# A graph layer's first attention group: node row and edge sources in one table, and one gather to a block instead of two

## The chip, the cores and the metric

The kernel runs on one core of a Trainium2 chip. The metric is the device time of one execution in microseconds (us); the time of the kernel before is the median of three runs. A profile is one execution recorded by the hardware profiler, with its own, longer time. The engines are named as in the profile: PE (matrix multiply), PEld (its weight loads), DVE (vector engine), ACT (scalar engine), POOL (GpSimd, which here issues all indirect DMAs), SP (the sync engine, which issues the plain DMAs). Each engine takes its instructions in program order, and so do POOL and SP with the DMAs that they issue.

## What is computed

A graph layer on 6,250 nodes with 256 features and 206,250 directed edges sorted by their destination. It adds to x an edge attention (8 heads of 32) and a linear attention, then a mixture of 8 experts with a capacity. The edge attention, which the change touches, is this (reference, cut):

```python
q = (feats @ Wq.T + bq).reshape(bs, NHEAD, HDIM).transpose(1, 0, 2)   # k, v likewise
r, c = (edge_index[:, 0], edge_index[:, 1])        # source, destination
sim = jnp.einsum('hed,hed->eh', q[:, c, :], k[:, r, :]) * scale
m = jax.ops.segment_max(sim, c, num_segments=bs)
p = jnp.exp(sim - m[c])
s = jax.ops.segment_sum(p, c, num_segments=bs)
attn = p / s[c]
agg = jax.ops.segment_sum(attn.T[..., None] * v[:, r, :], c, num_segments=bs)   # axes moved in the original
return agg @ Wo.T + bo
...
xn = _layernorm(x, axis=-1)
x = x + _L0_gnn_ref(xn, ...) + _L0_mix_ref(xn[None], ...)[0]
x = x + _L0_ffn_ref(_layernorm(x, axis=-1)[None], ...)[0]
```

For every node the rows k and v of its in-edges' sources (33 on average) have to be fetched; that is what the many gathers are for.

## The kernel before

**Blocks and groups.** The nodes are cut into 49 natural blocks of 128 (NB; one node to a partition). They form three groups of 21, 17 and 11 blocks (GROUPS). Within a group the nodes are sorted by falling number of edges, so that a sorted block needs few slots more than its nodes have edges. SLOTS holds the planned number of slots of each block: 62, 43, 41 and down to 24 in the first group, 725 slots there, 1,714 in all.

**The prologue** (L382 to L578) walks the natural blocks b = 0 to 48. For each: two matmuls give the block's k and v rows (L548, `rows_of(b + 2)`), DVE scales them into a tile kv (L562, one of six buffers of pool ap6), and SP stores kv into the DRAM table kv_tab (L565). After every fourth block SP also loads the next rows of x and of the transposed x (`load_x`, L409 and L213), and ACT takes the sums for the layer norm. Beside it `index_step(b)` (L528) finds where each node's edges begin. The edge list is cut into rows of 62 entries. For a set of 7 blocks (GB) POOL gathers one such row for each node (`row_gathers`, L504, tile part, two buffers), DVE counts the entries below the node's number (`in_rows`, L515 to L519) and writes the node's first edge into st_nat. The sets are handled at b = 8, 13, 18, ... (`due`); at the step for set k the gathers for set k + 2 are issued. From b = 24 on, `rank_group(0)` sorts the first group's nodes, one step to a block; its end (L371 to L378) gives, for each sorted place, the node (node_ri, node_x), its first edge (start_ri), its number of edges (deg_r) and its norm (rstd_r).

**The attention loop** (L1602 to L1655) goes over the sorted blocks in `order`, in units of at most 20 slots, each in chunks of at most 5 slots. For each chunk DVE multiplies the gathered k by the queries (L1621) and reduces (L1622); one unit later it weighs v (L1550) and PE sums it into pa (L1554). Jobs of the other stages (sorting the later groups, linear attention, routing, experts) are put between by a planned pace (`background`).

**The gathers.** `gather_to` (L648) runs six chunks ahead of DVE. For each slot of a chunk POOL issues one indirect DMA of 128 rows of 2 KB from kv_tab into a chunk buffer kvg (L662; RING = 10 buffers). When a block begins, it first issues two gathers for the block after it: `sources` (L600) fetches the sources of its edges from the list src, as many as it has slots, into idx (L605; pool cp3, three buffers); `queries` (L611) fetches the nodes' rows of x into the upper half of qs (L615; pool cp4, four buffers). The kv gathers take their row numbers from idx; `query_steps` makes the queries from qs.

**Waits and lanes.** In the built program each DMA carries one of eight completion lanes of its queue, taken in turn, and the next DMA of a lane waits until the last one of it is complete. A buffer that is written again waits, on the issuing engine, for whoever read it last; a read of an index tile by a gather counts as ended when that gather is complete.

Of the kernel before, what the change touches and what calls it, by code (L numbers as in the profile page):

```python
# [9 lines left out]
F32 = mybir.dt.float32  # L10
BF16 = mybir.dt.bfloat16
I32 = mybir.dt.int32
# [6 lines left out]
P = 128  # L19
# [9 lines left out]
GROUPS = (21, 17, 11)  # L29
# [15 lines left out]
def planned_slots(n_nodes, n_edges, groups):  # L45

    lam = max(1.0, n_edges / n_nodes - 1.0)  # L50
    pm = [math.exp(-lam)]
    for k in range(1, 1000):
        pm.append(pm[-1] * lam / k)
    more = [sum(pm[k:]) for k in range(len(pm))]
    out, b0 = [], 0
    for g in groups:
        m = min(n_nodes - b0 * P, g * P)
        for j in range(g):
            k = 1
            while True:  # L60
                p = more[k]
                if (m * p <= 0.005) if j == 0 else (m * p + 2.0 * math.sqrt(m * p * (1 - p)) <= P * j):
                    break
                k += 1
            out.append(k)
        b0 += g
    return out
# [3 lines left out]
def gps_layer(  # L71
# [36 lines left out]
    nc = tc.nc  # L108
    N, D = x.shape
    E = n_edges  # L110
    NB = -(-N // P)
# [16 lines left out]
    SMAX = max(SLOTS)  # L128
# [11 lines left out]
    dram = ctx.enter_context(tc.tile_pool(name="dram", bufs=1, space=DRAM))  # L140
# [5 lines left out]
    xbufs = [dram.tile([TILES[g] * SIZE[g], XW], F32, name=f"xbuf{g}") for g in range(NG)]  # L146

    rbufs = [dram.tile([TILES[g] * SIZE[g], D], F32, name=f"rbuf{g}") for g in range(NG - 1)]

    agg_tab = dram.tile([NB * P, D], F32, name="agg_tab")  # L150
    xbuf = dram.tile([NX * C + NB * P, D], F32, name="xbuf")
# [5 lines left out]
    with tc.manual_schedule():  # L157
# [24 lines left out]
        st_nat = keep.tile([P, NB + 1], F32, name="st_nat")  # L182
        nc.vector.memset(st_nat, float(E))
        node_ri = keep.tile([P, NB], I32, name="node_ri")
        node_x = keep.tile([P, NB], I32, name="node_x")
# [31 lines left out]
        cp4 = mctx.enter_context(tc.tile_pool(name="c4", bufs=4))  # L217
        cp3 = mctx.enter_context(tc.tile_pool(name="c3", bufs=3))
        cp2 = mctx.enter_context(tc.tile_pool(name="c2", bufs=2))
# [50 lines left out]
        GB = 7  # L270
# [111 lines left out]
        with ExitStack() as actx:  # L382
            ap1 = actx.enter_context(tc.tile_pool(name="a1", bufs=1))
            ap2 = actx.enter_context(tc.tile_pool(name="a2", bufs=2))
# [69 lines left out]
            first_i = di[:, :TW].rearrange("p (r w) -> p r w", w=RW)[:, :, 0]  # L454
# [38 lines left out]
            def rows_of_nodes():  # L493
                nc.vector.tensor_tensor_scan(cnt1, ones[:, :NB], pc[:, 1, :], 0.0, op0=ALU.mult, op1=ALU.add)
                nc.vector.tensor_sub(cnt1, cnt1, pc[:, 1, :])
                nc.vector.tensor_add(cnt1, cnt1, pc[:, 0, :])
                nc.vector.tensor_scalar(cnt1, cnt1, -1.0, 0.0, op0=ALU.add, op1=ALU.max)
                nc.vector.tensor_copy(row_i, cnt1)
                nc.vector.tensor_scalar(cnt1, cnt1, float(RW), None, op0=ALU.mult)

            def row_gathers(b0):
                part = ap2.tile([P, GB, RW], I32, name="part")
                for b in range(b0, min(NB, b0 + GB)):
                    nc.gpsimd.indirect_dma_start(  # L504
                        out=part[:, b - b0, :], out_offset=None, in_=row_dst,
                        in_offset=bass.IndirectOffsetOnAxis(ap=row_i[:, b : b + 1], axis=0),
                    )
                got.append(part)

            def in_rows(b0):  # L510
                g = slice(b0, min(NB, b0 + GB))
                n = g.stop - b0
                part = got.pop(0)
                below = ap1.tile([P, GB, RW], F32, name="below")
                nc.vector.tensor_tensor(  # L515
                    below[:, :n, :], part[:, :n, :], node[:, g, None].to_broadcast([P, n, RW]), ALU.is_lt
                )
                nc.vector.tensor_reduce(cnt2[:, g], below[:, :n, :], AX.X, ALU.add)
                nc.vector.tensor_add(st_nat[:, g], cnt1[:, g], cnt2[:, g])  # L519
# [4 lines left out]
            due = {8 + 5 * k: k for k in range(NSET)}  # L524
            ranks = rank_group(0, rc, ap1, ap2)
            late_sets = []

            def index_step(b):  # L528
                if b == 1:
                    rows_of_nodes()  # L530
                    row_gathers(0)
                    row_gathers(GB)
                if b in due:
                    k = due[b]
                    in_rows(k * GB)
                    if k + 2 < NSET:
                        row_gathers((k + 2) * GB)
                if b >= 8 + 5 * (need0 - 1) + 1:
                    next(ranks, None)

# [14 lines left out]
            for b in range(NB):  # L555
                k = b // GX
                if b % GX == 0 and k + 1 < NGX:
                    stat_square(k + 1)
                if b % GX == GX - 1 and k + 1 < NGX:
                    stat_end(k + 1)  # L560
                kv = ap6.tile([P, 2 * D], F32, name="kv")
                nc.vector.scalar_tensor_tensor(  # L562
                    kv, done.pop(b), rstd[:, b : b + 1], bn, op0=ALU.mult, op1=ALU.add
                )
                nc.sync.dma_start(kv_tab[b * P : (b + 1) * P, :], kv)  # L565
                if b % GX == GX - 1 and k + 1 < NGX:
                    load_x(k + 3)
                    if k + 2 < NGX:
                        stat_sum(k + 2)
                rows_of(b + 2)  # L570
                if b == 4:
                    less_mean(wq, D)
                index_step(b)
# [13 lines left out]
            for b in order:  # L587
# [3 lines left out]
                for i in range(n_p):  # L591
                    n = cut[i + 1] - cut[i]
# [5 lines left out]
            idx_of, qs_of, kv_of = {}, {}, {}  # L598

            def sources(i):  # L600
                if i < NB:
                    b = order[i]
                    S = SLOTS[b]
                    idx = cp3.tile([P, SMAX], I32, name="idx")
                    nc.gpsimd.indirect_dma_start(  # L605
                        out=idx[:, :S], out_offset=None, in_=src[:, :],
                        in_offset=bass.IndirectOffsetOnAxis(ap=start_ri[:, b : b + 1], axis=0),
                    )
                    idx_of[b] = idx

            def queries(i):  # L611
                if i < NB:
                    b = order[i]
                    qs = cp4.tile([P, 2 * D], F32, name="qs")
                    nc.gpsimd.indirect_dma_start(  # L615
                        out=qs[:, D:], out_offset=None, in_=x[:, :],
                        in_offset=bass.IndirectOffsetOnAxis(ap=node_x[:, b : b + 1], axis=0),
                    )
                    qs_of[b] = qs

            def query_steps(b):
# [26 lines left out]
            def gather_to(k):  # L648

                nonlocal pool_at  # L650
                while pool_at < min(k, len(chunk_list)):
                    u, c = chunk_list[pool_at]
                    b, part, _, _, _, chunks = units[u]
                    i = order.index(b)
                    if c == 0 and part == 0 and i > 0:
                        sources(i + 1)
                        queries(i + 1)
                    j0, j1 = chunks[c]
                    kv = kvp.tile([P, W, 2 * D], F32, name="kvg")
                    kv_of[u, c] = kv  # L660
                    for j in range(j0, j1):
                        nc.gpsimd.indirect_dma_start(  # L662
                            out=kv[:, j - j0, :], out_offset=None, in_=kv_tab[:, :],
                            in_offset=bass.IndirectOffsetOnAxis(ap=idx_of[b][:, j : j + 1], axis=0),
                        )
                    pool_at += 1

            for i in range(2):
                sources(i)
                queries(i)  # L670
# [931 lines left out]
        for u, (b, part, n_p, s0, s1, chunks) in enumerate(units):  # L1602
            n = s1 - s0
# [621 lines left out]
```

## Time and profile before

| | |
|---|---|
| median of three runs | 2770.39 us (2766.16 to 2770.42) |
| profiled execution | 3178.49 us, of which the span from first to last instruction is 3176.7 us |
| mean granted PE clock in it | 0.846 |
| busy share of the span | PE 71%, DVE 69%, POOL 59%, PE loads 54%, ACT 24% |
| DMA, software queue (POOL's gathers) | 148,880 packets, 477.59 MB, 50.3% of 16 engines' span |
| DMA, hardware queue (SP's) | 108,220 packets, 231.24 MB, 20.7% |
| idx gathers (L605) | 49, from 114.3 to 2880.5 us, 944 ns each |
| query gathers (L615) | 49, from 115.6 to 2881.8 us, 946 ns each |
| row gathers of the prologue (L504) | 49, busy 46.41 us of POOL |

The profile's columns: a group of equal instructions stands as line, engine, operation, written tile <- read tiles, count, busy us and mean ns of one, then the idle time of the engine just before them and what ended most of it ("issue": nothing that the profile shows; "remote": something outside the engines' own instructions). [...] The profiled execution is 408 us longer than the median, so a stage's length in it is not its length in the runs. The page's own chain of waits names only the last few instructions, 0% of the span, so the reading goes by stages: the prologue to 140 us, the first group to about 1290 us, the later groups to about 2890 us, and the rest.

### The profile page before, as it was taken

Reading aid. Unit: us, or ns where it says so; the run is one execution under the profiler, and the core shown is the slowest. Engines: PE = TensorE matmul, PEld = TensorE weight load, DVE = VectorE, ACT = ScalarE, POOL = GpSimd, SP = SyncE. Lnnn points to the kernel's source line nnn. Section 1 sums busy time; section 2 is a strip of 40 time slices with the busy share of each in tenths; the row PEclk is TensorE's granted clock in tenths of the full one; section 3 lists DMA queues with packets and bytes.
Section 4 is the critical chain, followed back from the end, with each engine's and each line's share of the span. In section 5 each row is a group of like instructions: output and inputs, shape, how many; then the busy total and the mean of one; then the engine's idle time right before and its main releaser. Section 6 shows DMA issues by size and latency. Waiting matters only on the chain. (4 is left out here: it accounts for less than half of the span.)

```text
span 3176.7 us, 29837 instructions
## 1 busy us (share of the span) xinstructions
PE 2247.2 (71%) x8968; PEld 1721.8 (54%) x8968; DVE 2183.7 (69%) x3637; ACT 767.7 (24%) x2022; POOL 1870.1 (59%) x2026
## 2 busy tenths in 40 slices
PE   7636577767767567674548888889844479999847
PEld 3324344545545445553337677777633357777637
DVE  4758788878778668787947666666867546766621
ACT  5200233333333212220012222222200112222113
POOL 4356666666666655656676566666665665655411
PEclk9857788888889778887769899989967689999969
DMA  7556777777776666766687778777765778887475
GB/s 233 188 166 183 214 225 223 238 215 232 219 218 196 191 186 208 216 186 170 195 273 266 238 260 268 247 266 257 216 170 177 247 252 269 275 274 265 156 265 209
DMA packets 257274, 710.88 MB, mean 224 GB/s; under 512 B 42183, under 2 KB 92113, under 8 KB 245580
## 3 DMA queue, kind: packets, MB, share of 16 engines
q0 software_dynamic: 148880, 477.59, 50.3%
q1 hardware_dynamic: 108220, 231.24, 20.7%
q8 instruction: 76, 1.25, 0.2%
q14 instruction: 98, 0.80, 0.1%
HBM read 626.63 MB, written 82.06 MB: 223 GB/s over the span
## 5 line engine op out<-in xcount | busy, mean ns | idle before, releaser
L662 POOL DMA_INDIRECT kvg<-kv_tab,idx x1714 | 1628.5, 950 | 1024.3 <-issue 470.8
L1554 PE MATMUL pa<-kvg,ident 128*128 128x256 f32 x3428 | 1015.1, 452 | 578.0 <-DVE kvg L1550 374.6
L1554 PEld LDWEIGHTS pa<-kvg,ident 128*128 128x128 f32 x3428 | 758.0, 228 | 795.8 <-DVE kvg L1550 424.1
L1621 DVE TENSOR_TENSOR kvg<-kvg,qc 128x1024 f32<-128x1024 f32 (+1 forms) x381 | 513.7, 1348 | 104.4 <-issue 45.4
L1622 DVE TENSOR_REDUCE sim<-kvg 128x32 f32<-128x1024 f32 (+1 forms) x381 | 515.3, 1353 | 17.8 <-remote 4.7
L1550 DVE TENSOR_TENSOR kvg<-kvg,pr 128x1024 f32<-128x1024 f32 (+1 forms) x381 | 510.2, 1342 | 0.0
L1370 PE MATMUL bank<-xTe,wt 128*128 128x256 f32 x1088 | 269.0, 394 | 12.5 <-ACT xTe L1360 7.5
L1387 PE MATMUL bank<-wt,hTe 128*128 128x256 f32 x1088 | 266.8, 393 | 11.7 <-issue 11.7
L1370 PEld LDWEIGHTS bank<-xTe,wt 128*128 128x128 f32 x1088 | 212.7, 198 | 47.4 <-issue 9.3
L1387 PEld LDWEIGHTS bank<-wt,hTe 128*128 128x128 f32 x1088 | 211.6, 197 | 45.7 <-issue 16.5
L1376 ACT ACTIVATE hTe<-bank,wt 128x256 f32<-128x256 f32 x272 | 112.7, 470 | 319.0 <-PE bank L1370 131.6
L756 PE MATMUL bank<-wm,xTm 128*128 128x512 f32 x392 | 182.0, 608 | 0.9 <-issue 0.9
L1404 ACT ACTIVATE res<-bank,xt 128x256 f32<-128x256 f32 x68 | 32.2, 473 | 366.5 <-PE bank L1393 144.3
L756 PEld LDWEIGHTS bank<-wm,xTm 128*128 128x128 f32 x392 | 73.9, 199 | 74.6 <-issue 74.5
L1561 DVE TENSOR_REDUCE s<-pr 128x8 f32<-128x120 f32 (+8 forms) x108 | 30.4, 281 | 118.2 <-ACT pr L1653 71.4
L1579 DVE TENSOR_TENSOR acc<-acc,pa 128x256 f32<-128x256 f32 x59 | 24.9, 421 | 124.2 <-remote 99.5
L548 PE MATMUL pkv<-wn,xT 128*128 128x512 f32 x196 | 94.0, 632 | 14.2 <-issue 11.2
L765 ACT ACTIVATE sq<-bank 128x512 f32<-128x512 f32 x98 | 55.4, 594 | 199.7 <-PE pa L1554 72.5
L785 ACT ACTIVATE ck<-bank,rk 128x64 f32<-128x64 f32 x392 | 86.4, 350 | 29.3 <-DVE rk L782 12.5
L1407 DVE TENSOR_TENSOR res<-res,xt 128x256 f32<-128x256 f32 x79 | 33.3, 421 | 82.9 <-ACT res L1404 62.1
L773 DVE TENSOR_REDUCE rv<-sq 128x16 f32<-128x1024 f32 x49 | 59.4, 1212 | 43.1 <-ACT sq L765 37.8
L896 PE MATMUL bank<-ident,qs 128*128 128x128 f32 x56 | 14.2, 343 | 95.2 <-DVE qs L1587 40.2
(312 smaller groups left out, 2467.2 us busy)
## 6 DMA issues: line engine op xcount, KB each, us to landing
wt<-in_w_rows_dram SPq DMA_DIRECT2D x34, 1152.0 KB
wt<-in_w_rows_dram SPq DMA_DIRECT2D x34, 1028.0 KB
kvg<-kv_tab,idx POOLq DMA_INDIRECT x1714
xbuf<-zero SPq DMA_DIRECT2D x43, 514.0 KB
kvg<-in_w_rows_dram SPq DMA_DIRECT2D x11, 1152.0 KB
kv_tab<-kv SPq DMA_DIRECT2D x49, 256.0 KB
hx_tab<-hx SPq DMA_DIRECT2D x49, 256.0 KB
kvg<-in_w_rows_dram SPq DMA_DIRECT2D x11, 1028.0 KB
```

Of the source, the lines that this page charges most:

```text
L548: nc.tensor.matmul(done[b], xTs[b // GX][:, b % GX, c, :], wn[:, c, :], start=(c == 0), stop=(c == DC - 1))
L662: nc.gpsimd.indirect_dma_start(out=kv[:, j - j0, :], out_offset=None, in_=kv_tab[:, :], in_offset=bass.IndirectOffsetOnAxis(ap=idx_of[b][: ...
L756: nc.tensor.matmul(pm, xT_of[b][:, c, :], wmf[:, c, s * MI : (s + 1) * MI], start=(c == 0), stop=(c == DC - 1),)
L773: nc.vector.tensor_reduce(rv, sqs[b], AX.X, ALU.add)
L785: nc.scalar.activation(cks[b][:, h, :], pms[b][0][:, h * MD : (h + 1) * MD], AF.Copy, scale=rk[:, h : h + 1])
L1370: nc.tensor.matmul(ph[:, k, :], w[:, c, f * P : (f + 1) * P], T[t]["xT"][:, c, :size], start=(k == 0 and c == 0), stop=(k == 1 and c == DC ...
L1376: nc.scalar.activation(T[t]["hT"][:, f, :size], ph[:, k, :], AF.Relu, bias=w1_t[:, V1 + f : V1 + f + 1])
L1387: nc.tensor.matmul(py, T[t]["hT"][:, f, k * P : (k + 1) * P], w[:, f, :], start=(f == 0), stop=(last and f == FC - 1),)
L1550: nc.vector.tensor_tensor(vals, vals, v["pr"][:, j0 - s0 : j1 - s0, :, None].to_broadcast([P, m, GH, GD]), ALU.mult)
L1554: nc.tensor.matmul(v["pa"], ident, kv[:, j, D:], start=(j0 + j == s0), stop=(j0 + j == s1 - 1),)
L1621: nc.vector.tensor_tensor(keys, keys, qc[:, None, :].to_broadcast([P, j1 - j0, D]), ALU.mult)
L1622: nc.vector.tensor_reduce(sim[:, j0 - s0 : j1 - s0, :], keys.rearrange("p j (h d) -> p j h d", d=GD), AX.X, ALU.add)
```

## The change

The first group's two gathers to a block become one. A new DRAM table xs_tab has a row for each node of the first 21 natural blocks: its 256 values of x, and behind them the IW = 62 sources that begin at its first edge (1,272 bytes in all). It is filled in the prologue. The x part is one DMA from DRAM to DRAM (2,688 rows), issued by SP just ahead of the first kv store. The sources come in three sets of 7 blocks, at b = 8, 13 and 18: once a set's first edges are in st_nat, DVE copies them to integers (first_i, two buffers), POOL gathers 62 sources for each node, block by block (ids, one buffer of 7 blocks), and SP stores ids into the table's last columns. These gathers stand on POOL behind the row gathers of the same step, and the store stands on SP behind the kv store of the same step.

In the first group `sources` does nothing any more, and `queries` fetches a row of xs_tab into a wider qs; its last 62 columns serve as idx. The later groups keep both gathers, but idx now has two buffers (cp2) in place of three (cp3). In the built program the first gather of a set of ids waits for DVE's copy and, from the second set on, for the store of the set before it; the store waits for all the set's gathers; and 26 of the 28 remaining idx gathers wait on several or all of the eight lanes of POOL's queue, where they waited on one.

```diff
--- before.py
+++ after.py
@@ -146,6 +146,9 @@
     xbufs = [dram.tile([TILES[g] * SIZE[g], XW], F32, name=f"xbuf{g}") for g in range(NG)]
 
     rbufs = [dram.tile([TILES[g] * SIZE[g], D], F32, name=f"rbuf{g}") for g in range(NG - 1)]
+
+    IW = max(planned_slots(N, E, GROUPS)[: GROUPS[0]])
+    xs_tab = dram.tile([GROUPS[0] * P, D + IW], F32, name="xs_tab")
 
     agg_tab = dram.tile([NB * P, D], F32, name="agg_tab")
     xbuf = dram.tile([NX * C + NB * P, D], F32, name="xbuf")
@@ -524,6 +527,24 @@
             due = {8 + 5 * k: k for k in range(NSET)}
             ranks = rank_group(0, rc, ap1, ap2)
             late_sets = []
+            nc.sync.dma_start(xs_tab[:, :D], x[: GROUPS[0] * P, :])
+
+            def first_sources(b0):
+
+                g = slice(b0, min(GROUPS[0], b0 + GB))
+                n = g.stop - b0
+                first_i = ap2.tile([P, GB], I32, name="first_i")
+                nc.vector.tensor_copy(first_i[:, :n], st_nat[:, g])
+                ids = ap1.tile([P, GB, IW], I32, name="ids")
+                for i in range(n):
+                    nc.gpsimd.indirect_dma_start(
+                        out=ids[:, i, :], out_offset=None, in_=src[:, :],
+                        in_offset=bass.IndirectOffsetOnAxis(ap=first_i[:, i : i + 1], axis=0),
+                    )
+                nc.sync.dma_start(
+                    xs_tab[b0 * P : (b0 + n) * P, D:].rearrange("(t p) w -> p t w", p=P),
+                    ids[:, :n, :].bitcast(F32),
+                )
 
             def index_step(b):
                 if b == 1:
@@ -535,6 +556,8 @@
                     in_rows(k * GB)
                     if k + 2 < NSET:
                         row_gathers((k + 2) * GB)
+                    if k * GB < GROUPS[0]:
+                        first_sources(k * GB)
                 if b >= 8 + 5 * (need0 - 1) + 1:
                     next(ranks, None)
 
@@ -598,10 +621,10 @@
             idx_of, qs_of, kv_of = {}, {}, {}
 
             def sources(i):
-                if i < NB:
+                if GROUPS[0] <= i < NB:
                     b = order[i]
                     S = SLOTS[b]
-                    idx = cp3.tile([P, SMAX], I32, name="idx")
+                    idx = cp2.tile([P, SMAX], I32, name="idx")
                     nc.gpsimd.indirect_dma_start(
                         out=idx[:, :S], out_offset=None, in_=src[:, :],
                         in_offset=bass.IndirectOffsetOnAxis(ap=start_ri[:, b : b + 1], axis=0),
@@ -611,11 +634,19 @@
             def queries(i):
                 if i < NB:
                     b = order[i]
-                    qs = cp4.tile([P, 2 * D], F32, name="qs")
-                    nc.gpsimd.indirect_dma_start(
-                        out=qs[:, D:], out_offset=None, in_=x[:, :],
-                        in_offset=bass.IndirectOffsetOnAxis(ap=node_x[:, b : b + 1], axis=0),
-                    )
+                    row = cp4.tile([P, 2 * D + IW], F32, name="qs")
+                    qs = row[:, : 2 * D]
+                    if i < GROUPS[0]:
+                        nc.gpsimd.indirect_dma_start(
+                            out=row[:, D:], out_offset=None, in_=xs_tab[:, :],
+                            in_offset=bass.IndirectOffsetOnAxis(ap=node_ri[:, b : b + 1], axis=0),
+                        )
+                        idx_of[b] = row[:, 2 * D :].bitcast(I32)
+                    else:
+                        nc.gpsimd.indirect_dma_start(
+                            out=qs[:, D:], out_offset=None, in_=x[:, :],
+                            in_offset=bass.IndirectOffsetOnAxis(ap=node_x[:, b : b + 1], axis=0),
+                        )
                     qs_of[b] = qs
 
             def query_steps(b):
```

## The prediction

> **What bounds the kernel now.** First the page's list of groups, for the dearest line, then the busy time by stage. The columns of the second view are the stretch, its length, busy us (and instructions) of PE, PE loads, DVE, ACT and POOL, the granted clock, the DMA share and GB/s.
>
> ```profile
> L662 POOL DMA_INDIRECT kvg<-kv_tab,idx x1714 | 1628.5, 950 | 1024.3 <-issue 470.8
> ```
>
> ```profile
> 0.00:140.00 140.00, 108.63 (x298) 51.26 (x298) 81.05 (x195) 61.23 (x213) 52.73 (x62) 0.95 0.64 212
> 140.00:1290.00 1150.00, 747.70 (x2668) 537.23 (x2668) 895.68 (x1454) 314.28 (x822) 738.03 (x779) 0.82 0.70 208
> 1290.00:2890.00 1600.00, 1186.62 (x4926) 958.97 (x4926) 1090.17 (x1733) 321.26 (x774) 990.93 (x1075) 0.86 0.74 237
> ```
>
> A gather costs POOL 0.95 us of work and 0.30 us until the next may start (470.8 us of "issue" over 1454 waits): 1.25 us. With that, POOL is taken for 738 + 779 x 0.30 = 972 of the first group's 1150 us, 85%; DVE is busy for 78%. So who waits for whom? DVE's waits in the first group (total, times, longest):
>
> ```profile
> DVE acc L1579 <- remote: 56.9, 10, 8.1
> ...
> DVE kvg L1621 <- DMA kvg<-kv_tab,idx: 6.7, 3, 4.9
> ```
>
> DVE waited only 6.7 us for gathered rows, 4.9 of it for the very first chunk. The gathers run ahead; POOL itself waits for buffers, also in the later groups:
>
> ```profile
> POOL kvg L662 <- issue: 240.6, 774, 3.7
> POOL kvg L662 <- PE pa L1554: 130.7, 47, 8.7
> POOL kvg L662 <- remote: 72.9, 29, 4.8
> ```
>
> So POOL is not last in the attention loop: DVE, in step with PE and ACT, is. The prologue is different. The timeline (start, length, engine, line, what; in brackets the idle time before):
>
> ```profile
> 47.22 0.94 POOL L504 DMA_INDIRECT part<-in_dst_dram,row_i  x1 [0.30 <-issue]
> 53.93 0.94 POOL L504 DMA_INDIRECT part<-in_dst_dram,row_i  x1 [5.77 <-DVE below L515]
> ...
> 114.35 0.94 POOL L605 DMA_INDIRECT idx<-in_src_dram,start_ri  x1 [18.59 <-DVE rstd_r L377]
> ...
> 138.06 1.08 POOL L662 DMA_INDIRECT kvg<-kv_tab,idx  x1 [18.86 <-issue]
> ```
>
> The first kv gather stands still for 18.86 us although its sources were asked for at 114.35: it needs all of kv_tab, whose last store SP issued at 135.06. The stores of the 49 kv blocks (L562, L565) set the prologue's end, and all that follows starts from there.
>
> **Gathers removed in the first group.** 21 idx gathers go (L605; 944 ns and a gap of 0.30 each): 21 x 1.25 = 26 us of POOL. Two of them stand at 114 to 119 us, ahead of the wait to 138: worth 0. The others give POOL more of the slack that it already has. Bounds: 0, and -26 if POOL were last everywhere. By the 6.7 us that DVE waits for rows: 0. The row that is now fetched is longer (1,272 bytes for 1,024), but a gather of 248 bytes (L504, 0.94), of 1,024 (L615, 946 ns) and of 2,048 (L662, 950 ns) cost POOL the same, so it costs nothing there.
>
> The Trainium skill, "DMA: Bandwidth & Descriptors", section "Anatomy of one DMA — SWDGE (gpsimd) path", gives a fixed cost of about 2.0 us for each DMA whatever its size. By that, half as many query and source gathers would bring 21 x 2.0 = 42 us. But that is latency, and these are issued a whole block, some 33 gathers, before they are read; by the rows it is 1.25 us of an engine that waits anyway. I take the rows.
>
> **Gathers added in the prologue.** 21 ids gathers, in three sets of 7 behind the row gathers of the steps at b = 8, 13 and 18: 7 x 1.25 = 8.75 us of POOL each. Before, POOL has the next row set from 39.7 to 48.2 and only then idles. As built the order is: third row set to 48.5, ids 0 to 57.2, fourth row set to 66, ids 1 to 74.7, fifth row set to 83.5, ids 2 to 92.2, back to back. When do they land? The first chunk shows it:
>
> ```profile
> 141.95 0.95 POOL L662 DMA_INDIRECT kvg<-kv_tab,idx  x1 [0.30 <-issue]
> ...
> 145.70 1.22 DVE L1621 TENSOR_TENSOR kvg<-kvg,qc 128x1024 f32<-128x1024 f32 x1 [4.89 <-DMA kvg<-kv_tab,idx]
> ```
>
> The chunk's last gather left POOL at 142.90, and its reader started 2.8 us later. So the sets are in SBUF at 60, 77.5 and 95.
>
> **The store of ids, on SP: the term that decides.** Each set is written to xs_tab by a DMA in SP's queue, in program order: behind the kv store of b = 8, 13 or 18, ahead of the next ones. It must wait for its 7 gathers, and behind it wait kv stores 9 to 13, 14 to 18 and 19 onwards, and the loads of x and xT. SP is blocked from about 36 to 60, 63 to 77.5 and 80 to 95. kv has six buffers (ap6), so DVE gets six blocks past the last stored one: block 25 needs the store of block 19, which goes out at 95 and lands near 98. In the trace of before:
>
> ```profile
> 76.56 1.41 DVE L562 SCALAR_TENSOR_TENSOR kv<-pkv,rstd,bn 128x512 f32<-128x512 f32 x2
> ```
>
> These are blocks 24 and 25; block 25 starts at 77.2. That is 98 - 77 = 21 us late. Blocks 26 to 35 carry the rank steps of the first group with DVE 18.75 of 20 us busy (80 to 100 us), and 36 to 48 come every 1.72 us, PE's own pace, so nothing is caught up: **+21 us**. Bounds: if the prologue outside the profile runs at PE's pace from 13.4 us on, block 25 stands near 62 before and the loss is 36; if POOL issues without the gap, its 56 gathers from 22 take 53 us instead of 70 and the loss is about 5. I take 21, the row's.
>
> The rule that speaks against the change is on the same page and section: DMA engines do not wait on semaphores, the issuing sequencer does, before dispatch. If instead a DMA could be queued with its wait, SP would pass on and only POOL's 26 us would count; its last row set is read at b = 38 (117.8 us) and would land at about 113, so the sum would be 0. In the trace SP's waits are those of the rule (45.0 us at L565 for kv), so I take 21.
>
> **x into xs_tab.** One DRAM-to-DRAM DMA of 2.75 MB on SP, ahead of the first kv store. Between 115 and 120 us the DMAs moved 372 GB/s; at that rate it is 7.4 us of all engines. Below: 0, since it falls into 11 to 25 us, partly idle, and its backlog of kv stores lies under the SP block from 36 on. Above: 15, if reading and writing DRAM halves the rate. I take 0; the three copies of first_i (DVE, under 0.2 us each) are 0 under the same block.
>
> **Two idx buffers for three, in the groups after the first.** The gather into idx for block i+1 now reuses the buffer whose readers are the kv gathers of block i-1, issued just before it. As built it waits for all eight completion lanes (two blocks: for four or six), that is for every gather under way; before it waited for one lane. 26 of the 28 blocks have it: 2.8 - 0.3 = 2.5 us of POOL each, 65 us. Queued behind are the idx and query gathers and the next chunk's kv gathers, and DVE's L1621 waits for these. Cover: POOL's waits for buffers, 130.7 + 72.9 us and smaller ones, in a run-ahead of some five chunks of 8 us. Bounds 0 and +65; since DVE met missing rows at about 8 of some 200 chunks there, I take **+5**.
>
> **Sum** against the profiled execution: 3178.5 us (span 3176.7 and 1.8 around it) + 21 + 5 = 3204. The median of the runs is 2770.4, 408 us less, and I add the same 26 us: what is added is issue and landing time. **2796 us.**
>
> **The rivals.**
> - POOL is the bound outside the profile (22%). From 140 to 2890 POOL is taken for 1729 + 1854 x 0.30 = 2285 us; if the missing 408 us all come out of these 2750, POOL is at 98%. Against it: DVE's waits. Then the first group gains some 20 of its 26 us, the idx waits cost 50 of their 65, the prologue 25: 2825.
> - The faster one: POOL paces the first group alone, with its relief worth the whole 26 us, while the later idx waits stay hidden. It decides once the prologue's block costs under 26; at 10, because gathers issue quicker without the profile: 2770 - 26 + 10 = 2754 (9%). For it: 85% taken; against: three waits of DVE for rows.
> - The store on SP is hidden (9%): kv_tab is not what ends the prologue outside the profile, +3 remains: 2773. Against: 18.86 us at L662.
>
> The forecast has 60%. **Chances**, with 0.2% (5.5 us) as what a measurement can tell from none: faster 9, within 8, slower 83 of 100. The range is 2762 to 2852: below, part of the faster case; above, the POOL case with its terms at 36 and 65.
>
> **What would show it.** Right: in the timeline of after, SP's store of ids issued at about 60, 77 and 95; block 25 of kv near 98; first kv gather near 159; POOL's idx rows with a wait of about 2.5 us. Wrong: the first kv gather at 138 to 145, DVE waiting tens of us for gathered rows, or the first group shorter by 20 us or more.

## The result, and the profile after

The changed kernel takes 2856.5 us (median of 4 runs, 2854.53 to 2859.08) where the kernel before takes 2770.4 (4 runs, 2766.16 to 2770.6): a ratio of 1.0321, 95% interval 1.0309 to 1.0334. It is slower by 86 us; 26 were forecast.

Two things about the times come first. The profiled execution of the changed kernel took 2854.66 us, within the range of its runs: recording a profile costs no time that can be seen. And the kernel before needed 3,177 to 3,213 us in four of the five series of experiments below and 2,768 us in one. Each series ran on one chip, and these were five different ones. So the trace that the prediction read (3178.49 us) was hardly the runs' execution made longer by the recorder; it matches the chips on which this program needs some 400 us more. Below, **chip B** is the one of 2,768 us, which agrees with the runs of the result (2770.4; which chip those ran on is not recorded), and A1 to A4 are the others (3,213, 3,204, 3,177 and 3,208 us). Ratios are always taken within a series.

The timeline of the changed kernel, first SP's DMAs around the first store of ids (start, length, queue, line, what):

```profile
37.13 0.33 SPq L588 DMA_DIRECT2D kv_tab<-kv  x1
58.04 0.38 SPq L544 DMA_DIRECT2D xs_tab<-ids  x1
58.51 1.48 SPq L588 DMA_DIRECT2D kv_tab<-kv  x3
...
75.45 0.37 SPq L544 DMA_DIRECT2D xs_tab<-ids  x1
...
93.03 0.37 SPq L544 DMA_DIRECT2D xs_tab<-ids  x1
93.51 0.51 SPq L588 DMA_DIRECT2D kv_tab<-kv  x1
94.06 0.44 SPq L412 DMA_DIRECT2D kvg<-in_x_dram  x1
```

SP sends nothing for 20 us ahead of 58.04 and then three kv stores at once. DVE and ACT in the same stretch (in brackets the idle time before, and what ended it), and POOL's first kv gather:

```profile
62.41 0.75 DVE L585 SCALAR_TENSOR_TENSOR kv<-pkv,rstd,bn 128x512 f32<-128x512 f32 x1 [16.23 <-DMA kv_tab<-kv]
...
101.40 0.42 ACT L439 ACTIVATE junk<-kvg 128x256 f32<-128x256 f32 x1 [12.56 <-DMA kvg<-in_x_dram]
...
103.56 0.17 DVE L443 TENSOR_SCALAR sums<-sums 128x4 f32<-128x4 f32 x1 [10.91 <-ACT junk L439]
103.64 1.41 DVE L585 SCALAR_TENSOR_TENSOR kv<-pkv,rstd,bn 128x512 f32<-128x512 f32 x2
```

```profile
163.32 1.14 POOL L693 DMA_INDIRECT kvg<-kv_tab,qs  x1 [21.71 <-DMA kv_tab<-kv]
```

So the block on SP reaches DVE first through the six kv buffers, as forecast (16.23 us). At the second and third store it comes by another path: the rows of x that SP loads behind the store (94.06 us) arrive late, ACT's sums wait for them, and DVE for the sums. From 30 to 163 us DVE waits 17.7 us for kv buffers and 33.4 us for these sums. The kv gathers start at 163.3. What the page says of the remaining idx gathers, and of the time in which a gather lands:

```profile
L628 POOL DMA_INDIRECT idx<-in_src_dram,start_ri x28 | 26.5, 947 | 126.4 <-DMA kvg<-kv_tab,idx 85.6
...
kvg<-kv_tab,idx POOLq DMA_INDIRECT x989, 4.6
```

28 instructions of 0.947 us have 126.4 us of idle time ahead of them. The trace puts 85.6 of it down to gathers under way, whose median is 4.6 us from issue to landing, and 37.0 to nothing that it names. By the waits of the built program, 26 of the 28 wait for gathers under way.

### The profile page after: what moved, and what is told of

It reads as the page before. It is cut to its first block, busy times and chain, and to the rows that moved or that the text cites. A ratio compares the mean times of both kernels' runs of the same rounds, so it can differ in the third digit from the quotient of the medians.

```text
span 2852.8 us, 29942 instructions
## 1 busy us (share of the span) xinstructions
PE 2161.2 (76%) x8968; PEld 1669.6 (59%) x8968; DVE 2181.2 (76%) x3640; ACT 771.8 (27%) x2022; POOL 1871.4 (66%) x2026
## 3 DMA queue, kind: packets, MB, share of 16 engines
q8 instruction: 76, 1.25, 0.2%
## 5 line engine op out<-in xcount | busy, mean ns | idle before, releaser
L1585 PE MATMUL pa<-kvg,ident 128*128 128x256 f32 x3428 | 972.8, 438 | 470.7 <-DVE kvg L1581 470.2
L693 POOL DMA_INDIRECT kvg<-kv_tab,idx x989 | 941.3, 952 | 349.8 <-issue 256.9
L1585 PEld LDWEIGHTS pa<-kvg,ident 128*128 128x128 f32 x3428 | 727.1, 218 | 674.3 <-DVE kvg L1581 540.7
L693 POOL DMA_INDIRECT kvg<-kv_tab,qs x725 | 688.2, 949 | 251.5 <-issue 173.3
L1418 PE MATMUL bank<-wt,hTe 128*128 128x256 f32 x1088 | 257.8, 384 | 0.0
L1401 PE MATMUL bank<-xTe,wt 128*128 128x256 f32 x1088 | 254.5, 380 | 1.4 <-ACT xTe L1391 1.4
L1401 PEld LDWEIGHTS bank<-xTe,wt 128*128 128x128 f32 x1088 | 205.4, 191 | 30.0 <-ACT xTe L1391 1.9
L628 POOL DMA_INDIRECT idx<-in_src_dram,start_ri x28 | 26.5, 947 | 126.4 <-DMA kvg<-kv_tab,idx 85.6
L571 PEld LDWEIGHTS pkv<-wn,xT 128*128 128x128 f32 x196 | 39.9, 213 | 86.1 <-DVE kv L585 43.7
L507 POOL DMA_INDIRECT part<-in_dst_dram,row_i x49 | 46.5, 949 | 48.5 <-DVE cnt L502 20.1
```

The costliest lines, as they stand in the source:

```text
L571: nc.tensor.matmul(done[b], xTs[b // GX][:, b % GX, c, :], wn[:, c, :], start=(c == 0), stop=(c == DC - 1))
L693: nc.gpsimd.indirect_dma_start(out=kv[:, j - j0, :], out_offset=None, in_=kv_tab[:, :], in_offset=bass.IndirectOffsetOnAxis(ap=idx_of[b][: ...
L1401: nc.tensor.matmul(ph[:, k, :], w[:, c, f * P : (f + 1) * P], T[t]["xT"][:, c, :size], start=(k == 0 and c == 0), stop=(k == 1 and c == DC ...
L1418: nc.tensor.matmul(py, T[t]["hT"][:, f, k * P : (k + 1) * P], w[:, f, :], start=(f == 0), stop=(last and f == FC - 1),)
L1585: nc.tensor.matmul(v["pa"], ident, kv[:, j, D:], start=(j0 + j == s0), stop=(j0 + j == s1 - 1),)
```

## The experiments

From here a run is read by **stages**: to the first kv gather (the prologue), the first group (725 kv gathers), the second, the third, and the rest. Stages are taken from the start times of the gathers in the trace.

### The third index buffer

E1, e6, e14 and e17 are the changed kernel with idx in three buffers again, on four chips; e5 is the changed kernel itself beside e6. E2 and e15 are the kernel before with two buffers, and nothing else of the change. E0, e4 and e13 are the kernel before, profiled for its stages.

```diff
-                    idx = cp2.tile([P, SMAX], I32, name="idx")
+                    idx = cp3.tile([P, SMAX], I32, name="idx")
```

> The kernel before, unchanged, for a second profile: its first one took 3178 us where the runs take 2770, while the changed kernel's profile (2855) agrees with its runs. Theory (the added time is the SP block in the prologue plus the idx waits of the later groups): a span near 2770, the first kv gather at about 115 to 120 us, so that the changed kernel's 163 is some 45 us late, and the first group as long in both. Rival (the loss lies in the first group, in the gathers that now hang on a longer row): the first kv gather near 138 as in the first profile, and a first group some 40 us shorter than in the changed kernel.

> The changed kernel with three idx buffers again. Theory: the 26 waits of about 4 us for all gathers under way go, and with them half of the loss: 2857 becomes about 2815. Rival (these waits are hidden behind the buffers, as my prediction had it): about 2850. A first kv gather at 163 in both.

> The kernel before with two idx buffers and nothing else. Now 46 or so of 49 blocks have the wait. Theory: 40 us for 26 blocks gives about 70 for 46, so 2840, less if the first group has more slack than the later ones (2810). Rival (hidden): 2770 to 2778.

> The kernel before, profiled beside the next three so that its stages can be set against theirs on the same chip. Both theories: the first row gather of the attention loop starts at 137 to 139 us, and the first group then takes about 1,140 us on a chip that runs the kernel in 3,200 us, or about 970 us on one that runs it in 2,770 us.

> The changed kernel as it is. Theory A (three terms: the prologue loses about 25 to 32 us, the first group gains about 26 us because 21 gathers of 1.25 us leave POOL there and POOL paces it, and two index buffers cost 40 to 85 us in the later groups): 50 to 90 us over before, ratio 1.016 to 1.033. Theory B (what I predicted: prologue +21, later groups +5, first group 0): ratio 1.009.

> The changed kernel with three index buffers again, beside the changed kernel on one chip. Theory A: the later groups get back 40 to 85 us, ratio to before 0.998 to 1.004. Theory B: only 5 us come back, ratio 1.007.

> The kernel before, profiled. On a chip that runs it in about 2,770 us: first row gather at 115 to 123 us, first group 964 to 970 us, second and third together about 1,485 us. On one that runs it in about 3,200 us: 138 to 146 us and 1,135 to 1,150 us.

> The changed kernel with three index buffers. Theory A (two buffers cost the second and third group about 65 us where the chip is fast): 60 to 70 us under the changed kernel, 20 to 27 us over before, ratio 1.007 to 1.010 on a chip of 2,770 us; on one of 3,200 us 1.001 to 1.004. Theory B (what I predicted, 5 us for the buffers): 1.025 to 1.03 on the fast chip.

> The kernel before with two index buffers in place of three, and nothing else of the change. 47 blocks meet the drain instead of 26. Theory A: 26 blocks cost 65 us, so 47 cost 95 to 120 us, ratio 1.034 to 1.043 on a chip of 2,770 us (1.014 to 1.026 on one of 3,200 us, as measured). Theory B (5 us for 26): under 10 us, ratio under 1.004.

> The changed kernel with three index buffers. On a chip that runs the kernel before in about 2,770 us: Theory A (two buffers cost the later groups 65 us there) 2,785 to 2,797 us, ratio 1.006 to 1.010; Theory B (5 us) 2,845 to 2,855 us, ratio 1.027 to 1.031. On a chip of 3,200 us: 1.000 to 1.004 as before.

| kernel | chip | ratio to before (95%) | prologue | first | second | third | rest |
|---|---|---|---|---|---|---|---|
| before (e0) | A1 | one run | 137.8 | 1148.8 | 1007.1 | 723.3 | 203.7 |
| three idx (e1) | A1 | 1.0015 (0.9995 to 1.0035) | 169.9 | 1121.6 | 999.1 | 716.6 | 206.3 |
| before, two idx (e2) | A1 | 1.0203 (1.0142 to 1.0264) | 146.1 | 1179.6 | 1027.7 | 720.9 | 208.6 |
| before (e4) | A2 | one run | 145.9 | 1145.2 | 995.8 | 714.2 | 203.5 |
| changed (e5) | A2 | 1.0134 (1.0102 to 1.0165) | 170.0 | 1121.5 | 1019.1 | 730.5 | 200.4 |
| three idx (e6) | A2 | 1.0028 (1.0010 to 1.0046) | 172.4 | 1119.5 | 988.5 | 720.0 | 208.5 |
| before (e13) | A3 | one run | 144.3 | 1138.8 | 997.0 | 702.1 | 203.4 |
| three idx (e14) | A3 | 1.0014 (0.9994 to 1.0034) | 170.7 | 1114.8 | 995.9 | 707.6 | 200.8 |
| before, two idx (e15) | A3 | 1.0202 (1.0157 to 1.0246) | 139.6 | 1168.1 | 1011.1 | 722.9 | 207.2 |
| three idx (e17) | A4 | 1.0022 (0.9995 to 1.0048) | 170.6 | 1125.0 | 988.7 | 716.8 | 210.8 |

The buffer alone costs 34 us of time on A2 (3243.9 for 3210.2) with 26 blocks draining, and 64 and 71 us on A1 and A3 where 47 blocks drain. The theory of 5 us falls. With the third buffer back the change costs 0.1% to 0.3% on these chips: what the prologue loses (26 to 32 us) the first group gives back (24 to 27 us). The prediction had 21 us for the first and nothing for the second. POOL's waits in e15 (total, times, longest):

```profile
POOL idx L605 <- DMA kvg<-kv_tab,idx: 130.0, 31, 6.6
POOL idx L605 <- issue: 50.9, 14, 7.4
```

181 us over 45 gathers, 4.0 each; with three buffers (e13) the same instruction's larger waits are one of 18.5 for the ranks and 48 of 0.3.

### What the prologue loses, part by part (chip B)

Each of the three adds parts of the prologue's change to the kernel before; nothing reads the table. E8 adds the copy of x alone, e9 the 21 gathers of sources alone, e10 the gathers and their stores.

```diff
             late_sets = []
+            nc.sync.dma_start(xs_tab[:, :D], x[: GROUPS[0] * P, :])
```

That was e8; e9 and e10 have these lines, with `first_sources` as the change has it in e10 and without its DMA on SP in e9:

```diff
                         row_gathers((k + 2) * GB)
+                    if k * GB < GROUPS[0]:
+                        first_sources(k * GB)
```

> The kernel before with one DMA more: the copy of the first group's x rows into the table, issued on SP ahead of the block loop (2.75 MB read and 2.75 MB written). Nothing reads the table. Theory C (the copy takes DMA time that the block loop's loads and stores need): first row gather 10 to 20 us later than before's 138 to 146 us. Theory D (what I predicted for the copy: 0): within 3 us of it.

> The kernel before with the 21 gathers of sources in the prologue alone, three sets behind POOL's gathers of destination rows; no copy of x, no store of the sources, and nothing reads them. What I predicted (POOL has the room): first row gather within 3 us of before's. Rival (POOL's later gathers of destination rows are pushed back and DVE waits for them): 8 to 26 us later.

> The kernel before with the 21 gathers of sources and their three stores on SP in the block loop, without the copy of x; nothing reads the table. What I predicted (SP stands at each store until its gathers land, and the stores of the block rows behind it, so the sixth row buffer, so DVE): 15 to 25 us later than before, whole prologue loss. Theory C (the copy is most of it): 5 to 12 us later.

| kernel, chip B (before 2767.9) | us | prologue | first | second | third | rest |
|---|---|---|---|---|---|---|
| e8, copy of x | 2773.0 | 126.8 | 965.2 | 850.7 | 633.9 | 194.6 |
| e9, gathers | 2793.2 | 138.7 | 968.6 | 850.0 | 634.6 | 199.5 |
| e10, gathers and stores | 2814.7 | 163.0 | 966.1 | 853.1 | 631.7 | 199.0 |
| changed kernel (result, before 2770.4) | 2856.5 | 163.3 | 947.0 | 913.7 | 636.2 | 192.6 |

The kernel before was not profiled on chip B. As the first group and all that follows is nearly alike in e8 to e10 (2,644 to 2,653 us), the differences of the times are mostly the prologue's loss: copy +5.1, gathers +25.3, gathers and stores +46.8 us. (Taken from the three prologues, they put the first kv gather of before at 122, 113 and 116 us.) The stores thus add 21.5 to the gathers, and the copy, worth 5 alone by this count, adds nothing beside them (163.3 for 163.0). These are single runs, against a spread of 6 us in the seven runs of before, and the later stages differ by 8 us among them. So the split is rough: with the first kv gather of before at 113 to 122 us, the prologues themselves give the copy 5 to 14 us, the gathers 17 to 26 and the stores behind them 24.3 (163.0 for 138.7).

Why the gathers cost time at all is told by the last gather of the fifth row set on POOL, 24.7 us later in e9 than in e8, nearly 21 x 1.25 = 26 (timeline, e8 first and e9 second):

```profile
83.55 0.94 POOL L507 DMA_INDIRECT part<-in_dst_dram,row_i  x1 [0.30 <-issue]
```

```profile
108.29 0.94 POOL L507 DMA_INDIRECT part<-in_dst_dram,row_i  x1 [0.30 <-issue]
```

and by the busy time by stretch, of e8 again and of e9 (stretch, length, busy us and instructions of PE, PE loads, DVE, ACT, POOL, clock, DMA share, GB/s):

```profile
24.00:84.00 60.00, 54.35 (x136) 23.58 (x134) 38.13 (x87) 33.08 (x119) 44.35 (x47) 0.97 0.90 298
```

```profile
24.00:109.00 85.00, 67.51 (x171) 31.05 (x170) 48.76 (x118) 37.67 (x136) 64.27 (x69) 0.91 0.70 222
```

With 0.30 us to each instruction POOL is taken for 44.35 + 14.1 = 58 of 60 us without the gathers and for 64.27 + 20.7 = 85 of 85 with them. There was no room on POOL. In e9 DVE then waits for it, 13.5 us for destination rows and 4.7 at its cast into first_i, where e8 has no wait for such rows:

```profile
DVE below L518 <- DMA part<-in_dst_dram,row_i: 13.5, 5, 5.0
...
DVE first_i L536 <- DMA ids<-in_src_dram,first_i: 4.7, 1, 4.7
```

With the stores beside them this wait is gone: in e10 DVE stands for kv buffers and for the sums of late x rows, as in the changed kernel, and for destination rows 0.3 us:

```profile
DVE sums L443 <- ACT junk L439: 31.8, 6, 10.8
DVE kv L584 <- DMA kv_tab<-kv: 19.1, 1, 19.1
...
DVE below L518 <- DMA part<-in_dst_dram,row_i: 0.3, 1, 0.3
```

Blocks 24 and 25 start there 38 us later than in e8 (e8 first, e10 second), and the first kv gather 36 us later:

```profile
65.02 1.41 DVE L566 SCALAR_TENSOR_TENSOR kv<-pkv,rstd,bn 128x512 f32<-128x512 f32 x2
```

```profile
103.26 1.41 DVE L584 SCALAR_TENSOR_TENSOR kv<-pkv,rstd,bn 128x512 f32<-128x512 f32 x2
```

So 25.3 and 21.5 are what each part adds in this order, and not two delays that lie one behind the other: with both, the loss runs through SP's stores, which wait for the gathers.

### Versions that try to keep the gain

E3 is the changed kernel (two idx buffers) with ids in three buffers and their stores on SP only at b = 40:

```diff
+                if b == 40:
+                    store_sources()
```

E7, e11, e16 and e18 have three idx buffers, the copy and the stores behind SP's last kv store, and two gathers still for the first two sorted blocks. They differ in where the 21 gathers stand. In e7 all are at b = 28, behind POOL's last gather of destination rows:

```diff
-                    if k * GB < GROUPS[0]:
-                        first_sources(k * GB)
+                    if (k + 3) * GB == NB:
+                        for b0 in range(0, GROUPS[0], GB):
+                            first_sources(b0)
```

In e11 they stay where the change has them, with ids and first_i in three buffers. E16 and e18, one kernel on two chips, make one cast for all at b = 23, 14 gathers at b = 28 and 7 just ahead of the first kv gather:

```diff
+                    if k + 3 == NSET:
+                        first_sources(0, 2 * GB)
...
+            first_sources(2 * GB, GROUPS[0])
+            store_sources(2 * GB, GROUPS[0])
+            nc.sync.dma_start(xs_tab[:, :D], x[: GROUPS[0] * P, :])
```

> The changed kernel with the three stores of ids moved on SP from the steps b = 8, 13, 18 to b = 40 (three ids buffers, so that the gathers needn't wait for the stores); POOL's order is unchanged. Theory (SP's queue is blocked by those stores): the first kv gather goes from 163 to about 125, and the time to about 2815. Rival (POOL's 21 added gathers hold up the row gathers, whose counts DVE waits for): the first kv gather stays at 145 or later, and the time at 2835 or more.

> Three index buffers; the copy of x and the stores of the sources are issued on SP behind the last store of the block loop, the gathers of the sources behind POOL's last gather of destination rows, and the first two blocks of the first group still use two gathers each, so that nobody waits for the table. Theory A: the prologue's loss goes (first row gather at 138 to 145 us), the first group's gain of 19 gathers by 1.25 us = 24 us stays, later groups as before: 10 to 24 us under before, ratio 0.992 to 0.997. Theory B (the first group gains nothing): ratio 1.000 to 1.002.

> Three index buffers; gathers of the sources in their place in the block loop into three buffers, so that neither POOL's gathers nor DVE's casts wait; copy of x and the three stores on SP behind the last store of the block loop; the first two blocks of the first group still use two gathers each. Theory A with C (copy and stores in the loop cost the prologue, the first group gains 19 gathers by 1.25 us = 24 us): first row gather within 8 us of before's, whole 15 to 24 us under before, ratio 0.992 to 0.996. If the 21 gathers themselves cost the prologue: first row gather 20 us or more late again, ratio 0.999 to 1.002.

> Three index buffers; the first 14 gathers of sources behind POOL's last gather of destination rows, where POOL then stands 18.5 us for the ranks, the last 7 ahead of the first row gather, where POOL stands 18.9 us for the block rows; one cast; stores of the sources and copy of x on SP behind the last store of the block loop; the first two blocks keep two gathers. Theory A: prologue within 3 us of before's, the first group 15 to 20 us shorter, the rest as before: ratio 0.992 to 0.996. If the first group's gain in the changed kernel was only its late start made good: ratio 0.999 to 1.002.

> The source gathers in POOL's two gaps, the stores and the copy behind the block loop, three index buffers. On a chip of about 2,770 us: the first group 15 to 20 us shorter than 966 us, prologue 0 to 8 us longer than before's, ratio 0.992 to 0.998. On a chip of 3,200 us: 0.995 to 1.000 as before.

| kernel | chip | ratio to before (95%) | prologue | first | second | third | rest |
|---|---|---|---|---|---|---|---|
| e3 | A1 | 1.0117 (1.0067 to 1.0167) | 171.8 | 1124.1 | 1024.8 | 722.7 | 200.5 |
| e7 | A2 | 1.0007 (0.9982 to 1.0032) | 170.9 | 1121.1 | 1000.1 | 705.7 | 210.3 |
| e11 | B | 1.0097 (1.0080 to 1.0114) | 139.3 | 966.9 | 856.2 | 635.9 | 198.7 |
| e16 | A3 | 0.9974 (0.9948 to 0.9999) | 152.6 | 1117.4 | 1001.4 | 708.8 | 205.1 |
| e18 | A4 | 0.9991 (0.9966 to 1.0016) | 154.3 | 1131.4 | 998.2 | 710.1 | 210.6 |

E3 and e7 missed: the prologue stayed at 171. In e7 first_i has two buffers, and DVE stood at the third cast until the first set's gathers had landed (timeline of e7):

```profile
113.28 0.17 DVE L537 CAST first_i<-st_nat 128x7 int32<-128x7 f32 x1 [17.72 <-DMA ids<-in_src_dram,first_i]
```

In e3 DVE waits up to 9.7 us for kv buffers between 45 and 107 us, put down to something outside the engines' instructions; why stores without a block in front came free so late on that chip is not settled. So on the chips of 3,200 us the part of the stores isn't shown: without them in the loop the prologue is 171.8, with them 169.9 (e1).

E11 on chip B parts the two again: with the stores and the copy gone from the loop the prologue is 139.3, like the 138.7 of the gathers alone. But it gains nothing in the first group (966.9), and a stall of 16.13 us there stands against the 24 us of POOL that are saved. The three stores follow the copy of x in SP's queue, and DVE's next user of the memory of ids waits for them (timeline of e11):

```profile
171.65 0.44 DVE L330 TENSOR_TENSOR_SCAN sc<-ones,bank 128x136 f32<-128x136 f32 x1 [16.13 <-DMA xs_tab<-ids]
```

E16 places the gathers where POOL stood still anyway (18.5 us for the ranks, 18.9 for the last kv rows), and the stores ahead of the copy. Its prologue is 8 us longer than e13's on the same chip, its first group 21 us shorter; the median is 5 us under before's, and 5 us again in e18, whose interval holds 1. That is the best version found, at 0.1% to 0.3%. It did not run on chip B.

### Where the other 40 us come from

From e10 (2812.9 us of span) to the changed kernel (2852.8) only the idx buffer, the gathers of the first group and the copy differ. Busy time by stage, e10 and then the changed kernel (first, second and third group; columns as above):

```profile
163.00:1129.10 966.10, 697.41 (x2626) 504.66 (x2627) 890.33 (x1444) 313.18 (x817) 730.51 (x767) 0.87 0.81 244
1129.10:1982.20 853.10, 705.35 (x3089) 581.03 (x3088) 689.57 (x1101) 207.38 (x486) 620.57 (x671) 0.90 0.83 274
1982.20:2613.90 631.70, 509.91 (x2202) 416.02 (x2202) 455.18 (x722) 139.55 (x349) 431.37 (x466) 0.89 0.82 269
```

```profile
163.30:1110.30 947.00, 692.86 (x2598) 501.11 (x2598) 882.36 (x1434) 312.80 (x815) 709.91 (x748) 0.87 0.81 249
1110.30:2024.00 913.70, 732.93 (x3189) 602.22 (x3190) 717.04 (x1137) 212.59 (x498) 621.37 (x671) 0.90 0.78 257
2024.00:2660.20 636.20, 495.48 (x2136) 403.90 (x2135) 438.32 (x697) 137.18 (x341) 429.94 (x466) 0.87 0.80 266
```

With 0.30 us to each instruction POOL is taken for 961 of e10's 966 us in the first group (99%), 822 of 853 in the second (96%) and 571 of 632 in the third (90%). It is the bound of the first two groups here. On chip A3 it is taken for (729.9 + 230.4) of 1138.8 us in the first, 84%, the share that the prediction saw. So on chip B 19 instructions fewer (19 x 1.25 = 24 us of POOL) shorten the first group by 19.1 us, and the drains in the second group are paid for the most part. The waits of the changed kernel in the second group, POOL's and then DVE's:

```profile
POOL idx L628 <- DMA kvg<-kv_tab,idx: 50.6, 10, 7.6
POOL idx L628 <- issue: 32.4, 6, 7.8
```

```profile
DVE kvg L1652 <- DMA kvg<-kv_tab,idx: 38.2, 15, 7.0
```

In e10, with three buffers, the idx gathers of the whole run have no wait over 0.3 us but the first one's for the ranks, and DVE in the second group no wait for rows:

```profile
POOL idx L627 <- issue: 13.9, 46, 0.3
```

```profile
DVE kvg L1643 <- DMA kvg<-kv_tab,idx: 0.3, 1, 0.3
```

83 us of drains over 16 blocks, 5.2 each; POOL had 31 us to spare in e10's second group, the group is 60.6 us longer, and DVE waits 38.2 us for rows. In the third group, where POOL has a tenth to spare, 39 us of drains cost 4.5. Two buffers alone did not run on chip B, but e11, which has the table and three buffers there, bears this out: its second and third group take 856.2 and 635.9 us, 57.8 less than the changed kernel's. Altogether: first group -19.1, second +60.6, third +4.5, rest -6.4 (not explained), prologue +0.3 = +39.9; with the 46.8 of e10 that makes 87 of the 86 us.

## Why the prediction was wrong

The direction was right and the size was not: 26 us were forecast and 86 came. The step that failed lies under the sum. The trace's 408 us over the runs were left without a cause, and two things were carried from it into the runs: that POOL has room (taken for 85% of the first group, and for 99% on chip B), and the start of the prologue's delay (block 25 at 77 us, where e8 has 65.7). Two sizes fell besides: the gathers removed and the price of a drain.

- **What bounds the kernel.** "So POOL is not last in the attention loop" failed for the chip of the runs. On chip B the same POOL work lies in 965 us instead of 1,139 (e8, e13), and POOL is full (99%). The prediction's own rival (POOL is the bound outside the profile, 2825 us) named this and gave it 22%; its three terms, -20, +50 and +25, were measured as -19.1, +65.1 and +46.8, the last in part by SP's block.
- **Gathers removed, 0 (bounds 0 and -26).** Measured -19.1 on chip B. Even on the chips that the trace stood for it was -24 to -27 (e0 to e1, e4 to e6, e13 to e14), so the reading "DVE waited only 6.7 us for rows, hence 0" was wrong there too. It is no mere making good of the late start: in e16 the prologue loses 8 and the group gains 21. Why the gathers pay in full with POOL taken for 84% is not settled.
- **Gathers added in the prologue, 0 beside the stores.** Alone they are not free: +25.3 us (e9). The prediction's own schedule had POOL back to back from 39.7 to 92.2 us and asked only when the ids land, not who waits for the row gathers pushed back behind them. Only the other reading of the completion rule considered POOL's 26 us, and called them covered. Beside the stores DVE's wait for those rows is 0.3 us (e10), so there the term may have held.
- **The stores on SP, +21.** The mechanism was right and the size was not. Stores were forecast at about 60, 77 and 95 us and came at 58.0, 75.5 and 93.0; block 25 at 98, seen at 104.3; the first kv gather at 159, seen at 163.3. The start that they were set against failed: block 25 at 77 us is the trace's, and e8 on chip B has it at 65.7, so the delay is 38 us; the first kv gather stood at 113 to 122 us and not at 138, so the way to 163 is 41 to 50 us and not 21. The bound of 36, for block 25 near 62, named this case. That e10 lies 21.5 us over e9 is no proof of the 21: it is another difference, and the likeness is luck. Part of the path was other than forecast too: blocks 24 and 25 waited for the sums of late x rows (12.56 us on ACT, 10.91 on DVE), which the prediction names behind the store and gives no cost. On the chips of 3,200 us the stores came at 58 to 59, 81 to 82 and 99 to 103 us and the first kv gather at 170 to 172 (e1, e5, e6, e14, e17). The rule that the issuing sequencer waits, not the DMA, agrees with SP's 20 empty us ahead of 58.04.
- **x into xs_tab, 0.** Right beside the stores (163.3 us for 163.0); alone it took 5.1 us of time (e8, one run).
- **Two idx buffers, +5 (bounds 0 and +65).** This step failed: +65.1 in the second and third group (57.8 against e11). The term was mis-sized twice, and that it came out at its upper bound, 26 x 2.5, is luck. A drain was priced at 2.8 - 0.3 = 2.5 us from the first chunk, whose gathers met an empty queue; in full flow the median gather lands after 4.6 us, and the 26 idx gathers waited 126 us, 4.8 each. The fixed cost of about 2.0 us that the Trainium skill gives ("DMA: Bandwidth & Descriptors", section "Anatomy of one DMA — SWDGE (gpsimd) path") lies to the same side: the shortest landing of a kv gather in the changed kernel was 3.2 us. And they were taken to be covered by POOL's waits for buffers, 130.7 + 72.9 us in the trace read. On chip B these are smaller: 92.1 us for PE's pa in the second and third group of e8, of which 43.8 are left in the changed kernel. So some 48 of the drains' 126 us stand where POOL waited anyway, and most of the rest is time.

Predicted +26 is 21 + 5; measured +86 is 46.8 (the prologue's gathers and stores together) + 65.1 - 19.1 - 6.4 and a rounding.

## What to carry to other kernels

Before a trace is used, set its time against the runs': where they differ, the trace may belong to another chip, and an engine that has 15% of slack in it may have none in the runs; ask which stage an engine would fill if the time were the runs' own. Count POOL's time for gathers as work and gap (1.25 us each here), and where that fills a stage, price every instruction moved into it at its full value, in a prologue too. Where a store blocks a queue, ask of each transfer behind it who reads it, loads as well as stores. Giving up one buffer of an index tile makes its refill wait for all gathers under way: price the drain by the landing time under load, and never by a first transfer on an empty queue.

## What the runs showed of the hardware

One program on five chips took 2,768 us on one and 3,177 to 3,213 on four, with instructions of equal length in e8 and e13 (DVE's product of k and the queries 1,349 ns in both, a kv gather 952 and 953) and a PE clock of 0.884 against 0.843. PE's whole busy time is 2,150.7 against 2,245.9 us, 95 us apart (the matmul into pa 438 against 452 ns), so the clock alone doesn't account for 400. On the chips of 3,200 us many waits end on something that the trace does not name (151.1 us of POOL's for kvg in e13, none in e8); their pages give no landing times, so a DMA may stand behind some of them. The spread of runs is 1% to 2% there, and 0.2% on chip B. The cause stayed open. It matters for this change: the same edit cost 1.3% on A2 and 3.2% where the result was taken.
